# Last image of a four-layer convolution block: the row norms of the next chunk taken first in the output loop, and depthwise taps moved from TensorE to VectorE

## Chip, cores and metric

The kernel runs on one core of one Trainium2 chip. The metric is the device time of one launch in microseconds (us); less is better. All data are float32. The engines are called PE (TensorE, matrix products), DVE (VectorE), ACT (ScalarE), POOL (GpSimd) and SP (SyncE, whose queue issues most of the transfers). Each engine works through its own instructions in the order in which the program hands them over, and semaphores hold an instruction back until what it needs is there.

## What is computed

The input is a batch of 4 images with 256 channels of 64 x 64 pixels. Four layers follow each other, each as x = x + layer(groupnorm(x)):

- layer 0: a 3x3 convolution, then attention over all 4096 pixels of the image;
- layer 1: linear attention with root-mean-square norms at its input and at its output;
- layer 2: a depthwise 3x3 convolution whose nine taps per channel are generated from the image, then a 1x1 convolution with a generated 256 x 256 matrix;
- layer 3: a 1x1 convolution with a mixture of four matrices.

The change touches layers 1 and 2, for the last image only. Cut to what matters there, the reference is:

```python
# layer 1, at its end: w_out times the attended values, then a norm over the channels of each pixel
out = einsum('oc,bchw->bohw', w_out, out) + b_out
n   = sqrt(sum(out * out, axis=1))              # one number for each pixel
x   = x + out / max(n, 1e-12) * g_out * sqrt(256)

# layer 2: u is groupnorm(x); dk has 9 taps for each channel, pk is 256 x 256
dw = depthwise_conv_3x3(u, dk)
x  = x + einsum('bchw,boc->bohw', dw, pk) + bias

# layer 3 begins with groupnorm(x), and so with the mean and variance of what layer 2 wrote
```

## The kernel before, in words

**The whole.** The work of one image is a front (layer 0's convolution and projections), an attention, and a tail (the end of layer 0 and layers 1 to 3). The tail of image b and the front of image b+2 are woven into the attention of image b+1 as generators that are advanced in turns with it. The last image has no attention after it that could hide its tail, so its tail stands alone at the end of the program. Pieces of the last 1x1 convolution of the image before it (`held`, L1676 to L1680) are kept back and issued by `w.fill(n)` at places where the tail leaves PE idle; `w.settle()` issues the additions that belong to them.

**The order.** There is no scheduler: the instructions of each engine stand in the order in which the Python code issues them. Tiles come from rotating pools. All PSUM banks come from one pool of 8 (`bank`), handed out in turn, so a product has to wait until the user of the bank eight requests earlier is done.

**Layer 1's output loop (L1281 to L1338).** The 4096 pixels are taken in 8 chunks of 512. For each chunk:

- `outputs(c)` multiplies four blocks of 128 pixels with the folded output matrix into two banks (PE, L1287), and ACT squares each block and sums it over the channels into a column of `zr` (L1289);
- `root(zr)` bounds the sums from below on DVE (L1294) and raises them to the power -0.5 on POOL (L217, through `rsqrt`);
- `scaled` multiplies the blocks with that root: three on ACT (L1303), the fourth on DVE (L1305), which in the program waits for the third copy of ACT;
- `added(c, z, halves)` transposes the scaled blocks on PE (L1316), and for each half of the channels DVE adds them to the image (recorded at L127, the helper `stt`) and takes statistics (`bn_stats`, L1318).

The loop for the last image is L1322 to L1338. In iteration c it issues `outputs(c+1)`, `scaled` of chunk c, the first half of `added` of chunk c-1, `root` of chunk c+1, and the second half of `added` of chunk c-1. In iterations 2 and 4 one held piece (two products of 512 pixels, one bank) is issued at the end, and the addition to it follows one iteration later. What the loop leaves behind, statistics of the whole image, is needed by everything that follows.

**Layer 2 for the last image (`shared_out`, L1541 to L1591).** The image is cut in 4 chunks of 1024 pixels (16 rows), and the 256 channels in 2 halves; part i is chunk i // 2 and half i % 2. The nine taps of a part are computed in one of two ways:

- on DVE: ACT writes the centre tap (`centre`, L1452), and `taps` (L1481 to L1491) adds eight shifted copies with `stt`, one instruction of 1008 or 1024 elements for each. Parts 0, 2, 4, 6 and 7 are made so.
- on PE: `taps_by_products` (L1493 to L1509) multiplies with nine diagonal matrices (`diag`, written by ACT at L1548), accumulating in a bank of 512 pixels; ACT copies the bank out (L1508). It is a generator that stops after each product. Parts 1, 3 and 5 are made so: 3 parts, 2 banks, 9 products, 54 in all.

When both halves of a chunk are there, `point` issues the 1x1 convolution (PE, L1460, four products for each half of a chunk), and `pointwise_added` adds the result to the image on DVE with a sum (L1476) and squares it on ACT with a sum (L1478). These sums are the statistics from which layer 3 starts (`st()`, L1437). The generated matrix `pk` is put together on DVE by `mix_kernel` (8 instructions of 512 elements, recorded at L127). The order of all this is written out by hand at L1563 to L1591 with `go(i, n)` (n taps of part i on DVE) and `diagonal(n)` (n products on PE).

**Layer 3.** A short chain of small steps gives the mixed matrix `wm`; PE then works off the last three held pieces and 32 products of its own (L1660), and DVE adds and stores each (L1665, L1666).

Of the kernel before, what the change touches and what calls it, by code (L numbers as in the profile page):

```python
# [13 lines left out]
P = 128  # L14
NH = 2
HW = 64
N = HW * HW
CH = 1024
RB = 8
# [74 lines left out]
def conv_preact_fast(ctx: ExitStack, tc: tile.TileContext, guard, x, wc, wtpg, ww, wqkv, wout, w1cat, wd2,  # L94
# [3 lines left out]
    nc = tc.nc  # L98
# [21 lines left out]
    def bank(name):  # L120
        return pp.tile([P, 512], F32, tag="bank", name=name, bufs=8)
# [4 lines left out]
    def stt(o, a, s, b, op0, op1):  # L126
        nc.vector.scalar_tensor_tensor(o, a, s, b, op0, op1)  # L127
# [5 lines left out]
    xp = cp.tile([P, NH, HW + 2, HW], F32, name="xp")  # L133
# [60 lines left out]
    half = cp.tile([P, 8], F32, name="half")  # L194
# [52 lines left out]
    taps = wc_s.rearrange("p h (i j) o -> p h i (j o)", i=3)  # L247
# [913 lines left out]
    def linear_attention(w, b, big, qT, k4, st, sh, sums):  # L1161

        alone = sums is not None
        if alone:
# [80 lines left out]
        last = None  # L1245
        for c in range(NC):
# [10 lines left out]
            last = this  # L1257
# [35 lines left out]
        def root(zr):  # L1293
            nc.vector.tensor_scalar(zr, zr, 1e-24, None, ALU.max)  # L1294
            rsqrt(zr, zr)

        def scaled(zr, banks):
            z = k4("z").rearrange("p (j o) -> p j o", j=4)
            if alone:
                for j in range(4):  # L1300
                    src = banks[j // 2][:, j % 2, :]
                    if j < 3:
                        nc.scalar.activation(z[:, j, :], src, AF.Copy, scale=zr[:, j:j + 1])  # L1303
                    else:
                        nc.vector.tensor_scalar(z[:, j, :], src, zr[:, j:j + 1], None, ALU.mult)  # L1305
                return z
            for s in range(2):
                tt(z[:, bass.ts(s, 2), :], banks[s], zr[:, bass.ts(s, 2)].unsqueeze(2).to_broadcast([P, 2, NH * P]), ALU.mult)
            return z

        def added(c, z, halves=range(NH)):
            cols = bass.ts(c, 512)
            for h in halves:
                pt = bank("ps_zt")
                for j in range(4):
                    nc.tensor.transpose(pt[:, bass.ts(j, P)], z[:, j, bass.ts(h, P)], ident)  # L1316
                stt(big[:, h, cols], pt, gains[:, 1, h:h + 1], big[:, h, cols], ALU.mult, ALU.add)
                nc.vector.bn_stats(st[:, h, c, :], big[:, h, cols])  # L1318

        if alone:  # L1320

            this, last = outputs(0), None  # L1322
            root(this[0])
            for c in range(NC):
                after = outputs(c + 1) if c + 1 < NC else None
                z = scaled(*this)
                for h in range(NH):
                    if last is not None:
                        added(c - 1, last, (h,))
                    if h == 0 and after is not None:  # L1330
                        root(after[0])
                this, last = after, z
                w.settle()
                if c in (2, 4):
                    w.fill(1)
                yield 1
            added(NC - 1, last)
            w.fill(2)  # L1338
            return st

        last = None
        for c in range(NC):
# [5 lines left out]
            last = scaled(*zb)  # L1348
# [9 lines left out]
    TAPS = [(i, j) for i in range(3) for j in range(3) if (i, j) != (1, 1)]  # L1358

    def generated(w, b, big, k4, st, sh, diag):  # L1360
# [108 lines left out]
        def pointwise_added(c, res):  # L1469
            cols = bass.ts(c, 512)  # L1470
            for oh in range(NH):
                if diag is None:
                    tt(big[:, oh, cols], res[oh], big[:, oh, cols], ALU.add)
                    nc.vector.bn_stats(st[:, oh, c, :], big[:, oh, cols])
                else:
                    nc.vector.scalar_tensor_tensor(big[:, oh, cols], res[oh], 1.0, big[:, oh, cols], ALU.mult, ALU.add,  # L1476
                                                   accum_out=sums[:, 0, oh, c:c + 1])
                    nc.scalar.activation(junk(), big[:, oh, cols], AF.Square, bias=pivot[:, oh:oh + 1],  # L1478
                                         accum_out=sums[:, 1, oh, c:c + 1])

        def taps(i):  # L1481

            c, h = PARTS[i]
            dst = dw[i].rearrange("p (y x) -> p y x", x=HW)
            for ty, tx in TAPS:
                dx = tx - 1
                x0, x1 = max(0, -dx), min(HW, HW - dx)
                k = h * 9 + 3 * ty + tx
                stt(dst[:, :, x0:x1], xp[:, h, c * rows + ty:c * rows + ty + rows, x0 + dx:x1 + dx], dk[:, k:k + 1],
                    dst[:, :, x0:x1], ALU.mult, ALU.add)  # L1490
                yield 0.62  # L1491

        def taps_by_products(parts):  # L1493

            for i in parts:
                c, h = PARTS[i]
                dw[i] = k4("dw")
                for s in range(2):
                    ps = bank("ps_dw")
                    dst = ps.rearrange("p (y x) -> p y x", x=HW)  # L1500
                    for n, (ty, tx) in enumerate([(1, 1)] + TAPS):
                        dx = tx - 1
                        x0, x1 = max(0, -dx), min(HW, HW - dx)
                        y0 = (2 * c + s) * RB + ty
                        nc.tensor.matmul(dst[:, :, x0:x1], diag[:, 3 * ty + tx, :], xp[:, h, y0:y0 + RB, x0 + dx:x1 + dx],  # L1505
                                         start=(n == 0), stop=(n == 8))
                        if n == 8:
                            nc.scalar.copy(dw[i][:, bass.ts(s, 512)], ps)  # L1508
                        yield  # L1509

        def mix_kernel(slices, js):

            for j in js:
                stt(pk, slices[j // 2][:, j % 2, :], pb[:, R + j:R + j + 1], pk, ALU.mult, ALU.add)
# [26 lines left out]
        def shared_out():  # L1541

            slices = [load_wp2(j) for j in range(R // 2)]
            yield from w.pending()
            products = taps_by_products([2 * c + 1 for c in range(N // CH - 1)])
            dw[0] = centre(0)
            for k in range(9):
                nc.scalar.activation(diag[:, k, :], ident, AF.Copy, scale=dk[:, 9 + k:10 + k])  # L1548
            on_vector = {i: taps(i) for i in (0, 2, 4, 6, 7)}

            def go(i, n):
                for _ in range(n):
                    next(on_vector[i])

            def diagonal(n):
                for _ in range(n):
                    next(products)

            def point(c):
                d = [dw[2 * c + h] for h in range(NH)]  # L1560
                return [(2 * c + s, pointwise_products(s, d)) for s in range(2)]

            dw[2] = centre(2)  # L1563
            diagonal(24)
            go(0, 8)
            w.settle()
            mix_kernel(slices, range(0, R // 2))
            go(2, 3)
            mix_kernel(slices, range(R // 2, R))
            go(2, 5)  # L1570
            dw[4] = centre(4)
            res = point(0)
            diagonal(12)
            pointwise_added(*res[0])
            go(4, 1)
            pointwise_added(*res[1])
            go(4, 7)
            dw[6], dw[7] = centre(6), centre(7)
            res = point(1)
            diagonal(18)  # L1580
            go(6, 1)
            pointwise_added(*res[0])
            go(6, 2)
            pointwise_added(*res[1])
            go(6, 5)
            go(7, 8)
            res = point(2)
            pointwise_added(*res[0])
            res = res[1:] + point(3)
            for r in res:  # L1590
                pointwise_added(*r)  # L1591

        if diag is None:
            yield from in_order(range(len(PARTS)))
# [752 lines left out]
```

## Time and profile before

| | |
|---|---|
| three timed executions | 3084.27, 3085.98 and 3086.03 us, median 3085.98 |
| the profiled execution | 3084.23 us, of which the profile's span is 3082.4 us |
| busy share of the span | PE 97%, DVE 69%, ACT 38%, POOL 4% |
| granted TensorE clock over the span | 0.993 |
| output loop of the last image | 2899.17 us (first product) to 2941.91 us (first step after its statistics) |
| depthwise stage of the last image | 2954.15 us (first centre tap) to 3033.55 us (end of its last square) |
| products of layer 3 and end | from 3039.41 us |

A row of the profile names the source line, the engine, the operation, and the tiles that it writes and reads. Operations issued by a helper carry the helper's line: L127 is `stt`, L124 is `tt`, L217 is `rsqrt`. A float32 product appears as two records of PE, so "x48" in a row of PE is 24 products; a transpose is one record. The chain of waits follows the work that ended last backwards from its end: at each step it goes to what released the instruction, or to the instruction ahead of it on the same engine. In the rows of the stages, each engine's busy time in a stretch is followed by its count of instructions, and PEclk is the TensorE clock that was granted.

### The profile page before, as it was taken

The numbers are of one execution on the slowest core, as the hardware profiler recorded it, in microseconds if no ns is written. First come the engines' busy times: TensorE is split into PE (matmuls) and PEld (weight loads), VectorE is DVE, ScalarE is ACT, GpSimd is POOL, SyncE is SP. The second block draws the span as 40 slices with busy tenths as digits, with TensorE's granted clock in tenths as the row PEclk, the third lists the DMA queues.
The fourth block names the chain that finished last, engine by engine and source line by source line (L and its number), as shares of the span: only waits on it lengthen the run. The fifth ranks groups of instructions, "written<-read, shape, count | busy, mean of one in ns | idle before, by whom it ended". The sixth has DMA issues, their size and how long they took to land.

```text
span 3082.4 us, 24468 instructions
## 1 busy us (share of the span) xinstructions
PE 3000.3 (97%) x8606; PEld 1483.7 (48%) x8606; DVE 2128.5 (69%) x2780; ACT 1162.0 (38%) x2155; POOL 132.1 (4%) x178
## 2 busy tenths in 40 slices
PE   6899999999999999999999999999999999999998
PEld 3454555445554444444565444444546544444643
DVE  8747777853547996777536797678563569876485
ACT  2334333353555332223364532222436453334621
POOL 0100000000010000000011000000001100000100
PEclk9999999999999999999999999999999999999999
DMA  5233111122100023113300102311420000022021
GB/s 219 84 101 137 34 48 32 34 52 73 57 11 28 14 75 122 39 40 66 116 1 11 35 7 82 123 45 38 96 82 14 18 28 28 14 82 89 8 69 66
DMA packets 61089, 178.45 MB, mean 58 GB/s; under 512 B 6560, under 2 KB 16544, under 8 KB 56736
## 3 DMA queue, kind: packets, MB, share of 16 engines
q1 hardware_dynamic: 56928, 160.04, 15.1%
q0 software_dynamic: 4032, 16.78, 2.9%
q8 instruction: 70, 1.15, 0.2%
q14 instruction: 59, 0.48, 0.1%
HBM read 115.45 MB, written 78.12 MB: 63 GB/s over the span
## 4 chain that ended last, share of the span: by engine, by line
PE 77%; DVE 16%; issue 5%; ACT 1%; POOL 0%; DMA 0%; POOLq 0%; DVEq 0%; ACTq 0%
PE pf L984 22%; PE py L1040 22%; PE ps_qkv L1201 5%; PE ps_conv L512 4%; PE ps_tp L926 4%; DVE dw L127 4%; PE ps_ex L1660 4%; DVE tot L124 3%; PE ps_pw L1460 3%; PE ps_conv L584 2%; PE ps_g L931 2%; PE ps_wy L1021 2%; PE ps_o L1287 1%; PE ps_dw L1505 1%; DVE big L127 1%
## 5 line engine op out<-in xcount | busy, mean ns | idle before, releaser
L985 ACT ACTIVATE pr<-pf 128x512 f32<-128x512 f32 x1024 | 603.9, 597 | 1195.4 <-PE pf L984 1147.9
L984 PE MATMUL pf<-tpg 128*128 128x512 f32 x2048 | 968.9, 595 | 2.9 <-ACT pr L985 2.9
L1040 PE MATMUL py<-pr,tpg 128*128 128x512 f32 x2048 | 962.3, 592 | 2.5 <-ACT pr L985 2.3
L124 DVE TENSOR_TENSOR tot<-tot,pr 128x1024 f32<-128x1024 f32 x448 | 546.3, 1219 | 174.1 <-ACT pr L985 172.5
L1040 PEld LDWEIGHTS py<-pr,tpg 128*128 128x128 f32 x2048 | 388.6, 190 | 494.6 <-issue 477.6
L984 PEld LDWEIGHTS pf<-tpg 128*128 128x128 f32 x2048 | 382.0, 190 | 438.4 <-issue 412.6
L127 DVE SCALAR_TENSOR_TENSOR dw<-xp,dk,dw 128x1008 f32<-128x1008 f32 x208 | 263.0, 1268 | 9.9 <-ACT dw L1452 7.0
L512 PE MATMUL ps_conv<-v,u 128*128 128x512 f32 x384 | 171.0, 593 | 3.6 <-DVE v L124 3.6
L1201 PE MATMUL ps_qkv<-wqkv_s,xg 128*128 128x384 f32 x384 | 129.9, 487 | 0.0
L124 DVE TENSOR_TENSOR tpg<-ps_g,bg_s 128x512 f32<-128x512 f32 x32 | 22.1, 692 | 145.2 <-PE ps_g L931 145.2
L926 PE MATMUL ps_tp<-big,wtpg_s 128*128 128x512 f32 x256 | 117.7, 603 | 3.0 <-ACT big L684 3.0
L512 PEld LDWEIGHTS ps_conv<-v,u 128*128 128x128 f32 x384 | 72.6, 190 | 96.5 <-issue 89.8
L217 POOL TENSOR_TENSOR rstd<-rstd,half 128x2 f32<-128x2 f32 x24 | 17.6, 731 | 2342.1 <-DVE rstd L365 2225.2
L1013 DVE RECIPROCAL inv<-pss 128x512 f32<-128x512 f32 x31 | 103.9, 3352 | 5.5 <-PE pss L996 5.5
L1460 PE MATMUL ps_pw<-dw,pk 128*128 128x512 f32 x224 | 101.3, 592 | 0.0
L1201 PEld LDWEIGHTS ps_qkv<-wqkv_s,xg 128*128 128x128 f32 x384 | 72.2, 190 | 53.6 <-issue 9.8
L1220 DVE TENSOR_REDUCE qs<-qk 128x16 f32<-128x512 f32 x24 | 16.5, 686 | 117.4 <-ACT qk L1214 117.4
L927 ACT ACTIVATE tpg<-ps_tp,btp_s 128x512 f32<-128x512 f32 x64 | 43.8, 687 | 119.2 <-PE ps_tp L926 119.2
L926 PEld LDWEIGHTS ps_tp<-big,wtpg_s 128*128 128x128 f32 x256 | 47.8, 194 | 54.9 <-issue 50.4
L1289 ACT ACTIVATE junk<-ps_o 128x256 f32<-128x256 f32 x128 | 49.2, 385 | 63.9 <-PE ps_o L1287 56.3
L1214 ACT ACTIVATE qk<-ps_qkv,rinv 128x256 f32<-128x256 f32 x96 | 45.6, 475 | 72.4 <-PE ps_qkv L1201 60.0
L124 DVE TENSOR_TENSOR v<-ra 128x1024 f32<-128x1024 f32 x58 | 69.5, 1220 | 0.4
(369 smaller groups left out, 3132.7 us busy)
## 6 DMA issues: line engine op xcount, KB each, us to landing
xp<-in_x_dram SPq DMA_DIRECT2D x16, 1024.0 KB, 6.3
wy_d<-wt SPq DMA_DIRECT2D x32, 512.0 KB, 3.0
wy<-wy_d SPq DMA_DIRECT2D x32, 512.0 KB, 4.9
out_dram<-res SPq DMA_DIRECT2D x64, 256.0 KB, 2.0
xs_d<-big POOLq DMA_DIRECT2D x24, 512.0 KB, 11.1
u<-filters SPq DMA_DIRECT2D x48, 256.0 KB, 2.5
xs<-xs_d SPq DMA_DIRECT2D x24, 512.0 KB, 6.1
u<-rows_d SPq DMA_DIRECT2D x36, 256.0 KB, 3.1
```

What stands on the lines that cost most here:

```text
L124: nc.vector.tensor_tensor(o, a, b, op)
L127: nc.vector.scalar_tensor_tensor(o, a, s, b, op0, op1)
L512: nc.tensor.matmul(ps[oh], u(oh, h), v[:, bass.ts(h, 512)], start=(h == 0), stop=(h == NH - 1))
L584: nc.tensor.matmul(ps[:, bass.ts(oh, IY * IX)], u[i][:, h, bass.ts(oh, P)], v[:, i, bass.ts(h, IY * IX)], start=(h == 0), stop=(h == NH - 1))
L926: nc.tensor.matmul(ps, wtpg_s[:, h, k, :], big[:, h, cols], start=(h == 0), stop=(h == NH - 1))
L984: nc.tensor.matmul(pf, phi[:, bass.ts(2 * m + s, P)], theta[:, bass.ts(q, 512)], start=True, stop=True)
L985: nc.scalar.activation(pr[:, bass.ts(s, 512)], pf, AF.Exp)
L1013: nc.vector.reciprocal(inv, pss)
L1040: nc.tensor.matmul(py, g[:, bass.ts(2 * m + s, P)], probs[i][:, bass.ts(s, 512)], start=(m == 0 and s == 0), stop=(m == NM - 1 and s == 1))
L1201: nc.tensor.matmul(ps[:, 0:3 * HID], xg[:, h, bass.ts(j, P)], wqkv_s[:, h, :], start=(h == 0), stop=(h == NH - 1))
L1460: nc.tensor.matmul(ps, pk[:, h * NH * P + oh * P:h * NH * P + (oh + 1) * P], dw[h][:, bass.ts(s, 512)], start=(h == 0), stop=(h == NH - 1))
L1660: nc.tensor.matmul(ps, wm[h][:, bass.ts(oh, P)], big[:, h, bass.ts(c, 512)], start=(h == 0), stop=(h == NH - 1))
```

## The change

It has two parts, both in the tail of the last image.

In the output loop `root` of chunk c+1 is issued directly after `outputs(c+1)`, ahead of `scaled` of chunk c, and both halves of `added` of chunk c-1 follow together.

In the depthwise stage

- part 1 is made by PE from the centre and six taps, and its last two taps are added by DVE (`go(1, 2)`); PE so has 50 diagonal products in place of 54, and the calls of `diagonal` ask for 27, 5 and 18 in place of 24, 12 and 18;
- part 7 is made by DVE in two pieces of 8 rows (8 instructions of 504 or 512 elements for each piece) in place of 8 instructions of 16 rows;
- the last chunk's 1x1 products are issued one channel half and one piece at a time (`half(s, h)`): three of the four groups ahead of the second piece's taps in the program, the fourth after them; the additions of chunk 2's first half are issued between the two pieces, those of its second half after them.

```diff
             for c in range(NC):
                 after = outputs(c + 1) if c + 1 < NC else None
+                if after is not None:
+                    root(after[0])
                 z = scaled(*this)
-                for h in range(NH):
-                    if last is not None:
-                        added(c - 1, last, (h,))
-                    if h == 0 and after is not None:
-                        root(after[0])
+                if last is not None:
+                    added(c - 1, last)
                 this, last = after, z
...
-        def taps(i):
+        def taps(i, some=TAPS, over=slice(0, CH // HW)):
 
             c, h = PARTS[i]
-            dst = dw[i].rearrange("p (y x) -> p y x", x=HW)
-            for ty, tx in TAPS:
+            dst = dw[i].rearrange("p (y x) -> p y x", x=HW)[:, over, :]
+            for ty, tx in some:
...
-            products = taps_by_products([2 * c + 1 for c in range(N // CH - 1)])
+            products = taps_by_products([(1, TAPS[:6]), (3, TAPS), (5, TAPS)])
...
-            on_vector = {i: taps(i) for i in (0, 2, 4, 6, 7)}
+            on_vector = {i: taps(i) for i in (0, 2, 4, 6)}
+            on_vector[1] = taps(1, TAPS[6:])
...
             dw[2] = centre(2)
-            diagonal(24)
+            diagonal(27)
             go(0, 8)
             w.settle()
             mix_kernel(slices, range(0, R // 2))
             go(2, 3)
             mix_kernel(slices, range(R // 2, R))
+            go(1, 2)
             go(2, 5)
             dw[4] = centre(4)
             res = point(0)
-            diagonal(12)
+            diagonal(5)
...
             go(6, 5)
-            go(7, 8)
+
+            ends = [taps(7, TAPS, slice(s * RB, (s + 1) * RB)) for s in range(2)]
+            for _ in ends[0]:
+                pass
             res = point(2)
+            banks = [[bank("ps_pw") for _ in range(NH)] for _ in range(2)]
+
+            def half(s, h):
+                for oh in range(NH):
+                    nc.tensor.matmul(banks[s][oh], pk[:, h * NH * P + oh * P:h * NH * P + (oh + 1) * P],
+                                     dw[6 + h][:, bass.ts(s, 512)], start=(h == 0), stop=(h == NH - 1))
+
+            half(0, 0)
+            half(0, 1)
+            half(1, 0)
             pointwise_added(*res[0])
-            res = res[1:] + point(3)
-            for r in res:
-                pointwise_added(*r)
+            for _ in ends[1]:
+                pass
+            half(1, 1)
+            pointwise_added(*res[1])
+            for s in range(2):
+                pointwise_added(6 + s, banks[s])
```

More of the change, by code (lines that the diff above doesn't have):

```diff
@@ L1488, in taps @@
                 k = h * 9 + 3 * ty + tx
-                stt(dst[:, :, x0:x1], xp[:, h, c * rows + ty:c * rows + ty + rows, x0 + dx:x1 + dx], dk[:, k:k + 1],
+                y = c * rows + ty
+                stt(dst[:, :, x0:x1], xp[:, h, y + over.start:y + over.stop, x0 + dx:x1 + dx], dk[:, k:k + 1],
                     dst[:, :, x0:x1], ALU.mult, ALU.add)
@@ L1493, in taps_by_products @@
         def taps_by_products(parts):
-            for i in parts:
+            for i, some in parts:
                 c, h = PARTS[i]
@@ L1500, in taps_by_products @@
                     dst = ps.rearrange("p (y x) -> p y x", x=HW)
-                    for n, (ty, tx) in enumerate([(1, 1)] + TAPS):
+                    for n, (ty, tx) in enumerate([(1, 1)] + some):
                         dx = tx - 1
@@ L1505, in taps_by_products @@
                         nc.tensor.matmul(dst[:, :, x0:x1], diag[:, 3 * ty + tx, :], xp[:, h, y0:y0 + RB, x0 + dx:x1 + dx],
-                                         start=(n == 0), stop=(n == 8))
-                        if n == 8:
+                                         start=(n == 0), stop=(n == len(some)))
+                        if n == len(some):
                             nc.scalar.copy(dw[i][:, bass.ts(s, 512)], ps)
```

## The prediction, made before the changed kernel was run

> **What bounds the kernel now.** I read the share of busy time first, then the last 180 us in stretches, because the change lies only there, and then the chain of waits and the engines' timelines inside the stretches. PE is busy for 97% of the span, but not evenly:
>
> ```profile
> 2900.00:2925.00 25.00, 22.41 (x104) 15.64 (x103) 14.09 (x28) 18.65 (x71) 5.95 (x6) 1.00 0.06 22
> 2925.00:2950.00 25.00, 18.42 (x86) 9.49 (x86) 19.44 (x43) 7.78 (x23) 2.86 (x5) 0.80 0.11 37
> ...
> 2975.00:3000.00 25.00, 25.00 (x60) 11.18 (x59) 21.86 (x26) 4.97 (x12) 0.00 (x0) 1.00 0.00 1
> 3000.00:3025.00 25.00, 25.00 (x60) 11.05 (x60) 23.92 (x29) 6.67 (x14) 0.00 (x0) 1.00 0.00 0
> ```
>
> The columns are the stretch, its length, and busy time of PE, weight loads, DVE, ACT and POOL. In the output loop (2899 to 2942) no engine is full. In the depthwise stage (2954 to 3033) PE is full, and DVE nearly so. The chain of waits names the loop's cause:
>
> ```profile
> 2928.31 0.08 DVE zr L1294
> ...
> 2928.55 1.02 POOL zr L217
> ...
> 2929.59 1.22 ACT rt L1303 x3
> ...
> 2930.91 0.48 DVE rt L1305
> 2931.39 0.67 DVE tpg L127
> ...
> 2932.08 0.69 DVE st L1318
> 2932.78 0.08 DVE zr L1294
> ```
>
> This is a ring through four engines: root on DVE to POOL 0.30, POOL and handing on 1.04, ACT's three copies up to DVE's fourth 1.31, that copy 0.40, the addition 0.78, the statistics 0.61, then the next root: 4.46 per chunk. It closes only because the root stands on DVE behind the previous chunk's copy and addition.
>
> In the depthwise stage the timelines of DVE and ACT show:
>
> ```profile
> 3000.65 1.27 DVE L127 SCALAR_TENSOR_TENSOR dw<-xp,dk,dw 128x1008 f32<-128x1008 f32 x1 [3.33 <-ACT dw L1452]
> ...
> 3013.19 10.43 DVE L127 SCALAR_TENSOR_TENSOR rt<-xp,dk,rt 128x1008 f32<-128x1008 f32 x8
> ...
> 3031.63 0.69 DVE L1476 SCALAR_TENSOR_TENSOR tpg<-ps_pw,tpg 128x512 f32<-128x512 f32 x1 [1.02 <-PE ps_pw L1460]
> ```
>
> DVE once waits 3.33 for a centre tap, which stands on ACT behind the copy of PE's part 3 (2995.74) and four squares; and its last additions wait for PE, 1.02 each. So PE ends this stage.
>
> [...] the centre tap above waits 3.33 us behind work it doesn't need. [...] a chained addition of 512 elements takes 3.02 / 4 = 0.755 (the `pk` row, 2968.32 to 2971.34), one of 1008 or 1024 takes 10.35 / 8 = 1.294. [...] 0.50 granted from 2930.8 to 2941.0 and from 3036.6 to 3043.4.
>
> **Part 1, the root first.** No instruction is added; POOL gets its eight powers earlier, and no DMA moves past anything. The ring opens: root c+1 needs only the squares of chunk c+1. New on DVE is the wait: the fourth copy of chunk c and both additions of chunk c-1 now stand behind root c+1, hence behind those squares, and the transposes and later banks wait for these. Three limits are left. DVE alone: 4.46 less its idle 1.14, about 3.24 to 3.3 per chunk (plus 0.66 where a held piece is added). ACT alone: four squares 2.03 and three copies 1.09, 3.12. And banks: a chunk's products start when an addition two chunks back frees a bank. The trace has that sequence once: products 2921.99, squares 2923.10, copies 2925.13, fourth copy 2926.44, that is 4.45; from there to the end of the second addition 2.54; 7.0 for two chunks, 3.5 each. A held piece puts 1.72 of PE ahead of the next products.
>
> The walk of the fourth copies, from chunk 1 (2908.62, unchanged, since ACT was busy with squares until then):
> - chunk 2: DVE-bound, +3.2, 2911.9.
> - chunk 3: its squares wait for products of chunk 4, which follow the held piece (ends 2911.64): squares from 2912.8, copies 2914.7, 2916.0.
> - chunk 4: DVE-bound with a held addition, +3.9, 2919.9.
> - chunk 5: the second held piece waits for a copy of chunk 4 (2918.65); products 2920.4, squares 2921.5, copies 2923.5, 2924.8.
> - chunk 6: +3.9, 2928.7. Chunk 7: +3.2, 2931.9.
>
> Before, chunk 7 was at 2935.37; what follows (6.5 to the last statistics) keeps its shape. Gain 3.5. Ends: 5.5 if all of DVE's six waits go (1.11, 1.14, 0.49, 1.14, 0.49, 1.14); 1.4 if PE's clock halves inside the loop (rival below).
>
> **Part 2, the depthwise stage.** PE: 54 products took 20.39 + 10.19 + 15.29 = 45.87, 0.85 each; four fewer are 3.4 less. DVE gets two taps more (2.55 net of overlap 2.45), and 16 half taps at 0.755 (12.0) for 8 at 1.294 (10.35), 1.6 more. No trace row has half taps of 8 rows; the `pk` row is the nearest in length and chaining. From below 0.65 (half a full tap), from above 1.29 (no cheaper than a full one). I take 0.755.
>
> Walked in the old trace's times (part 1 only shifts them). PE: 27 products end at 2981.0; the first 1x1 needs part 1's two taps, done on DVE at 2980.7: no wait, but the cover is only 0.3, beyond which a late DVE costs one for one. 1x1 to 2987.9, 5 products to 2992.1, 1x1 to 2999.0, 18 products to 3014.2, 1x1 of chunk 2 to 3021.1, three groups of the last chunk to 3026.3. DVE: the two taps push it to 2999.8 where it waited for the centre tap; ACT, now freed 3.4 earlier, has that ready at 2997.5, so the wait of 3.33 is gone: DVE runs 0.9 ahead and starts part 7 at 3012.3. First piece 3018.3, two additions 3019.5, second piece 3025.4. PE's last group runs 3026.3 to 3028.0, so PE no longer ends the stage. DVE's six last additions run 3025.4 to 3029.1 without waiting. Next late is ACT: six squares at 0.845 from 3026.2 (0.78 after the first addition starts, as at 3023.54), end 3031.3. Before: 3033.55. Gain 2.25. The other instructions (copies, centres, squares) keep number and order; moved squares are hidden under PE's products, and would cost at most their 0.85 each.
>
> **After it.** Layer 3's chain (3033.55 to 3039.41) and PE's last products shift unchanged: the mixed matrix is ready at 3044.4, PE reaches it at 3046.6 behind held pieces. PE idles 8 to 9 us there in both kernels, so its clock halves in both[...]. Output transfers (2.0 us to landing) follow as before; the loads of `pk`'s slices land ten us ahead of use.
>
> **Sum.** 3084.23 (span 3082.4 and 1.8 around it) - 3.5 - 2.25 = 3078.5. The profiled execution is 1.75 below the median of the timed ones; the four executions lie in two pairs, near 3084.25 and 3086.0. I lift the sum to their middle, 0.9: 3079.4.
>
> **Rivals.**
> - All of DVE's waits in the loop go (5.5): 3077.4. For it: ACT's 3.12 is below DVE's 3.3. Against: banks and held pieces. 0.12.
> - PE's clock halves inside the loop: two-chunk sequence 1.3 longer, 4.2 per chunk against 4.46, gain 1.4: 3081.5. For it: 0.50 was granted from 2930.8 on. Against: PE's work is denser now. 0.13.
> - The depthwise part gives nothing, ACT's squares or a missed cover of 0.3 taking the place of PE: 3081.6. For it: DVE and PE are both full. 0.10.
> - Slower: half taps cost as much as full ones[...]. Then 16 x (1.294 - 0.755) = 8.6 more on DVE, which ends the stage: 3088.0. It decides above 0.755 + 5.75 / 16 = 1.11 per half tap. Against: 0.755 for 512 elements. 0.05; that the stage slips by still more is 0.03 of these.
> - As worked out: 0.60, half above the line drawn next.
>
> **How the numbers follow.** A measurement of this kernel can tell about 0.2%, 6.2 us, so the line is 3079.8; the forecast lies 0.4 below it. Faster by more: 0.12 + 0.33 = 0.45. Within: 0.27 + 0.13 + 0.10 + 0.02 = 0.52. Slower by more: 0.03. The range leaves out the slow rival and the far ends: 3076.0 to 3083.5.
>
> **What would show it.** Right: roots no longer in the chain of waits for each chunk; fourth copies 3.2 to 4.9 apart; DVE without the wait at the centre tap of part 6; the last squares back to back on ACT, and PE ending before them; half taps near 0.755. Wrong: a PE wait ahead of the first 1x1, DVE's idle at a root, or half taps above 0.9.

## The result: 3081.7 us against 3086.1

| | before | after |
|---|---|---|
| median of the executions (20 each) | 3086.07 us | 3081.71 us |
| lowest and highest | 3083.42, 3086.70 | 3079.36, 3082.43 |
| the profiled execution, and its span | 3084.23, 3082.4 | 3079.89, 3078.1 |

The ratio is 0.9986, 95% interval 0.9980 to 0.9993: 4.4 us less. The executions of each kernel lie in two groups about 2.4 apart, before near 3083.8 and 3086.2, after near 3079.7 and 3082.0. Both medians fall in the upper group and both profiled executions in the lower one, so medians and profiles compare like with like.

The stretches of the changed kernel that answer to those of before (stretch, its length, then busy time of PE, weight loads, DVE, ACT and POOL, the granted clock, DMA):

```profile
2900.00:2925.00 25.00, 23.34 (x110) 16.76 (x108) 15.00 (x31) 20.06 (x77) 7.05 (x7) 1.00 0.06 22
2925.00:2950.00 25.00, 19.55 (x90) 9.43 (x89) 21.01 (x48) 8.06 (x20) 1.75 (x3) 0.86 0.26 80
2975.00:3000.00 25.00, 25.00 (x60) 11.05 (x59) 24.57 (x30) 6.64 (x12) 0.00 (x0) 1.00 0.00 1
3000.00:3025.00 25.00, 24.55 (x58) 10.64 (x56) 24.36 (x39) 8.00 (x19) 0.00 (x0) 1.00 0.00 0
```

In the depthwise stage DVE went from 21.86 to 24.57 busy in 25 us: its wait is gone. PE is for the first time not full there, 24.55 in the last row: it is done before the stage ends.

The chain of waits in the loop of the changed kernel (start, time, what; "x3" are three instructions):

```profile
2923.36 1.10 ACT z L1303 x3
...
2924.56 0.48 DVE z L1305
2925.04 0.67 DVE tpg L127
...
2927.73 0.73 DVE res L127
2928.46 0.08 DVE zr L1294
2928.54 0.39 DVE rt L1305
```

POOL's root is gone from it. Before, it stood in the chain in the last two turns (2928.55 and 2933.01), and ACT's copies waited for it, 1.34 or more, in five of the six turns from chunk 2 on. The root on DVE (L1294) now takes its 0.08 in passing, between two pieces of DVE's own work. What stays is DVE's own sequence, and ACT's copies where a held piece came first.

DVE's timeline of the changed kernel, in the loop and in the depthwise stage (start, busy time, and in brackets the idle time ahead of the instruction and what ended it):

```profile
2911.69 0.15 DVE L1294 TENSOR_SCALAR zr<-zr 128x4 f32<-128x4 f32 x1
2911.75 0.48 DVE L1305 TENSOR_SCALAR ra<-ps_o,zr 128x256 f32<-128x256 f32 x1
...
2915.85 0.48 DVE L1305 TENSOR_SCALAR z<-ps_o,zr 128x256 f32<-128x256 f32 x1 [0.79 <-ACT z L1303]
...
2924.56 0.48 DVE L1305 TENSOR_SCALAR z<-ps_o,zr 128x256 f32<-128x256 f32 x1 [1.00 <-ACT z L1303]
...
2996.10 1.26 DVE L127 SCALAR_TENSOR_TENSOR dw<-xp,dk,dw 128x1008 f32<-128x1008 f32 x1
...
3015.97 6.21 DVE L127 SCALAR_TENSOR_TENSOR rt<-xp,dk,rt 128x504 f32<-128x504 f32 x8
...
3027.97 0.19 DVE L1436 TENSOR_REDUCE both_m<-sums 128x4 f32<-128x32 f32 x1 [2.04 <-ACT junk L1477]
```

Chunk 2's copy (2911.75) follows its root without a wait; chunks 3 and 5, the ones that stand behind a held piece, wait 0.79 and 1.00. Part 6's first tap (2996.10) has no bracket: the wait of 3.33 is gone. Eight half taps take from 3015.97 to the next addition at 3022.11, 0.767 each. DVE's last 2.04 of idle is ended by ACT: the squares now end the stage.

The gain, followed through the traces by marks that both kernels have (us, before to after):

| mark | before | after | gain so far |
|---|---|---|---|
| fourth copy of chunk 7 | 2935.37 | 2931.61 | 3.76 |
| first centre tap of layer 2 | 2954.15 | 2950.51 | 3.64 |
| last square of layer 2 done (`both_m`) | 3033.55 | 3027.97 | 5.58 |
| first product with the mixed matrix | 3046.62 | 3042.18 | 4.44 |
| last product of PE that both have (`count`) | 3075.99 | 3071.55 | 4.44 |

So 3.64 came from the loop and 1.94 from the depthwise stage, and then 1.14 was given back between the last square and the mixed matrix, where nothing had been changed. PE's timeline there, first before:

```profile
3039.34 7.44 PE L1660 MATMUL ps_ex<-big,wmh 128*128 128x512 f32 x12
3046.62 3.60 PE L1660 MATMUL ps_ex<-tpg,wm 128*128 128x512 f32 x8
```

and after:

```profile
3033.97 8.37 PE L1679 MATMUL ps_ex<-big,wmh 128*128 128x512 f32 x12
3042.18 3.60 PE L1679 MATMUL ps_ex<-tpg,wm 128*128 128x512 f32 x8
```

The same twelve records of the held pieces take 8.37 in place of 7.44. The stretches say why. In both traces the granted clock changes eleven times, each a whole multiple of 3.41 us from the others; a stretch between two such instants is called a window from here on, and the row of instants the grid. Cut at the grid, before:

```profile
3033.22:3036.63 3.41, 0.77 (x4) 0.59 (x4) 1.85 (x13) 0.30 (x2) 0.00 (x0) 1.00 0.01 2
3036.63:3040.04 3.41, 1.80 (x7) 1.49 (x8) 0.93 (x8) 0.35 (x2) 0.70 (x1) 0.50 0.02 5
3040.04:3043.46 3.42, 3.42 (x5) 1.35 (x4) 3.20 (x10) 0.00 (x0) 0.00 (x0) 0.50 0.00 0
```

and after:

```profile
3026.30:3029.71 3.41, 0.38 (x2) 0.30 (x2) 1.09 (x8) 1.61 (x4) 0.00 (x0) 1.00 0.01 2
3029.71:3033.12 3.41, 1.18 (x6) 1.01 (x6) 1.24 (x9) 0.00 (x0) 0.70 (x1) 0.50 0.00 0
3033.12:3036.54 3.42, 3.08 (x5) 1.67 (x6) 2.18 (x9) 0.35 (x2) 0.00 (x0) 0.50 0.03 5
3036.54:3039.95 3.41, 3.41 (x5) 1.35 (x4) 3.11 (x7) 0.00 (x0) 0.00 (x0) 0.50 0.00 0
```

Read the last but two columns (the clock) against the first busy column (PE). Before, half clock covers two windows, of which the held products sit in the second and a little of the first: 4.1 us of slow products. After, PE ends its 1x1 convolution 7.0 us earlier (3024.55 against 3031.60) and the held products begin 5.4 earlier, but the windows of these two profiles stand at the same places, within 0.1. So the products begin 0.85 behind the start of a window in place of 2.71; half clock covers three windows, and the products lie in two of them: 6.0 us slow. The window in which they began, with PE busy for 3.08 of its 3.42, was followed by another at half clock.

### The profile page after: what moved, and what is told of

Same layout as the page of the kernel before. It is cut to its first block, busy times and chain, and to the rows that moved or that the text cites. A ratio compares the mean times of both kernels' runs of the same rounds, so it can differ in the third digit from the quotient of the medians.

```text
span 3078.1 us, 24460 instructions
## 1 busy us (share of the span) xinstructions
PE 2996.4 (97%) x8598; PEld 1482.2 (48%) x8598; DVE 2132.2 (69%) x2790; ACT 1161.6 (38%) x2155; POOL 132.1 (4%) x178
```

## The experiments

Theory: the loop's gain is the opened ring; the depthwise gain is PE's four products and DVE's wait; what is missing was taken by the clock at the restart. Rivals: the two parts overlap, the pieces of part 7 bring the gain, or the restart is slower for another reason.

The edits are shown cut, against the changed kernel where nothing else is said. The kernel before was timed again beside every run, with medians from 3084.59 to 3086.07, depending on how many of its executions fell in either group; the changed kernel was not, so a difference to its 3081.71 of less than about 1.5 says little by itself. The marks in the profiles are the finer measure.

**The root first, alone.** The depthwise stage is as before.

```diff
-            products = taps_by_products([(1, TAPS[:6]), (3, TAPS), (5, TAPS)])
-            on_vector = {i: taps(i) for i in (0, 2, 4, 6)}
-            on_vector[1] = taps(1, TAPS[6:])
+            products = taps_by_products([2 * c + 1 for c in range(N // CH - 1)])
+            on_vector = {i: taps(i) for i in (0, 2, 4, 6, 7)}
...
-            diagonal(27)
+            diagonal(24)
```

> The kernel before with the first part of the change alone. Theory (the two parts add, and what is left over is TensorE's clock at the restart of layer 3): the last fourth copy of the loop near 2931.6 in place of 2935.4, the depthwise stage as long as before (first centre tap to end of the last square 79.4 us), and 3.6 us less than before in all, because the restart falls so in the clock's windows that about 4 us of it are slow, as before. Rival (the first part's gain is given back later): less than 2 us of the 3.7 are left at the end.

Measured: 3082.63, ratio 0.9992 (0.9984 to 1.0001), the kernel before at 3085.49 beside it. Chunk 7's fourth copy at 2931.64, the depthwise stage 79.40 as before, the last product at 3072.46: 3.5 earlier than before. So in the profiles nearly all of the loop's 3.76 arrives when it is alone; half clock at its restart lasts two windows, as before, not three, and the twelve held records take 7.51 (before 7.44, after 8.37). The medians show 2.9, less than the 3.6 expected, with an interval that reaches 1.0001: the rival falls by the marks, not by the times.

**The depthwise part, alone.** The loop is as before.

```diff
-                if after is not None:
-                    root(after[0])
                 z = scaled(*this)
-                if last is not None:
-                    added(c - 1, last)
+                for h in range(NH):
+                    if last is not None:
+                        added(c - 1, last, (h,))
+                    if h == 0 and after is not None:
+                        root(after[0])
```

> The kernel before with the second part of the change alone. Theory: the loop keeps its 4.46 us per chunk; the depthwise stage is 1.9 us shorter; but the restart of layer 3 comes about 0.8 us after a window's begin, the clock stays at half for 6 us in place of 4, and only 1.0 us is left of the 1.9 at the end. Rival (the lost 1.0 us of the changed kernel belongs to the loop or to an interaction of the parts): 1.9 us less than before at the end.

Measured: 3083.15, ratio 0.9996 (0.9987 to 1.0004). The stage takes 77.46, 1.94 shorter, but the last product comes only 1.1 earlier: half clock at the restart lasts three windows (3032.97 to 3043.21), and the held products take 8.28. So of the two it is this part that brings the slower restart in the profiles. The held products begin 1.93 earlier than before, which puts them 1.03 behind the start of a window; with the first part alone they begin 3.59 earlier, about a whole window, and stand 2.58 behind one, nearly as before. The median lies 2.3 below that of the kernel before, but fell in the lower group, the other in the upper; group against group it is about 1, as in the marks.

**The taps moved, part 7 in one piece.** Root first and the two taps on DVE are kept; the ending is the old one.

```diff
-            on_vector = {i: taps(i) for i in (0, 2, 4, 6)}
+            on_vector = {i: taps(i) for i in (0, 2, 4, 6, 7)}
...
-            ends = [taps(7, TAPS, slice(s * RB, (s + 1) * RB)) for s in range(2)]
-            for _ in ends[0]:
-                pass
+            go(7, 8)
             res = point(2)
...
             pointwise_added(*res[0])
...
+            res = res[1:] + point(3)
+            for r in res:
+                pointwise_added(*r)
```

> The changed kernel with part 7 in one piece and the old ending, two taps still on VectorE. Theory A (moving the taps is what pays[...]): walked from the trace of after, VectorE ends part 7 1.4 us sooner than in two pieces, TensorE's last products end near 3025.9, the last square near 3027.9, the same as in two pieces; total within 0.5 us of the changed kernel. Theory B (the pieces are what takes TensorE off the end of the stage): 1.5 to 2 us slower than the changed kernel.

Measured: 3081.31, ratio 0.9983 (0.9976 to 0.9990), in two groups, 3077.3 to 3077.8 and 3080.9 to 3082.0. The stage takes 76.84, 0.6 less than with two pieces. DVE's timeline of this kernel:

```profile
3010.75 10.43 DVE L127 SCALAR_TENSOR_TENSOR rt<-xp,dk,rt 128x1008 f32<-128x1008 f32 x8
...
3027.55 0.69 DVE L1475 SCALAR_TENSOR_TENSOR tpg<-ps_pw,tpg 128x512 f32<-128x512 f32 x1 [1.02 <-PE ps_pw L1459]
```

PE still ends the stage here: the last addition waits 1.02 for it, the one before 0.99. The pieces take those two waits away, 2.0, and cost 16 x 0.767 - 10.34 = 1.9 of DVE, so the last addition starts 74.65 after the first centre tap with them and 74.92 without. But with the pieces ACT still has squares to do when the additions end: the stage ends 2.81 after the last addition's start with them, 1.92 without. The profiled execution fell in the upper group and shows, besides, a window of half clock (2942.04 to 2945.45) over the small products of layer 2 ahead of this stage.

**The pieces, without the moved taps.**

```diff
-            products = taps_by_products([(1, TAPS[:6]), (3, TAPS), (5, TAPS)])
+            products = taps_by_products([(1, TAPS), (3, TAPS), (5, TAPS)])
...
-            diagonal(27)
+            diagonal(24)
...
-            go(1, 2)
             go(2, 5)
...
-            diagonal(5)
+            diagonal(12)
```

> The changed kernel with part 1 made by TensorE alone (54 diagonal products), part 7 in two pieces. Theory A: TensorE has its 3.4 us back and ends the stage again; the stage is about as long as in the kernel before (79.4 us), the total 1.5 to 2 us above the changed kernel unless the restart falls better in the clock's windows. Theory B (the pieces pay): within 0.5 us of the changed kernel.

Measured: 3083.45, ratio 0.9995 (0.9987 to 1.0003). The stage takes 79.79, against 79.40 of before: the pieces by themselves bring nothing, and what the depthwise part gains comes from the moved taps. The twelve held records take 7.23 (before 7.44, after 8.37).

**Warm products at the restart.** Products that nobody reads keep PE busy from its last 1x1 convolution to the held pieces.

```diff
             half(1, 1)
+            warm(512, 512, 512, 512, 512)
...
+    def warm(*widths):
+        ps = bank("ps_warm")
+        for n in widths:
+            nc.tensor.matmul(ps[:, 0:n], ident, tpg[:, NH, 0:n], start=True, stop=True)
...
-        mv, gm, rstd = yield from group_finish(st, avg8, 1e-5, sh)
+        mv, gm, rstd = yield from group_finish(st, avg8, 1e-5, sh,
+                                               (lambda: warm(384), lambda: warm(512, 128)) if held is None else ())
...
+        if held is None:
+            warm(256)
```

> The changed kernel with nine more products into banks that nobody reads, issued where TensorE has nothing to do between the last depthwise product and the restart of layer 3 (five of 512 columns first, then four of 128 to 512 between the small products). Theory (the restart of layer 3 loses half of its 5.9 us at half clock): full clock there, the last held pieces end 2.5 to 3.0 us earlier, total 2.5 to 3 us below the changed kernel. Rival (the restart is bound by the mixed matrix, or the late end comes from something else than the clock): no gain, or a loss of up to 0.5 us from the added products.

Measured: 3080.94, ratio 0.9987 (0.9981 to 0.9994), only 0.8 below the changed kernel. The condition `held is None` holds for the first two images as well, so the products also ran inside the attentions, and the last image's loop starts 4.8 later: the total is no test. The tail is: no half clock (1.00 granted from 3030 to 3042, where the changed kernel has 0.59), held products 5.42, and from the last square to the mixed matrix 10.65 in place of 14.21, so 3.6 us of the restart, as this profile of the changed kernel has it, are the clock's.

**The same in the last image only,** against the run just shown.

```diff
-                                               (lambda: warm(384), lambda: warm(512, 128)) if held is None else ())
+                                               (lambda: warm(384), lambda: warm(512, 128)) if b == B - 1 else ())
...
-        if held is None:
+        if b == B - 1:
             warm(256)
```

> The changed kernel plus unread warm products at the end of the depthwise stage and between the small products of layer 3's chain, in the last image only (five of 512 columns, then 384, then 512 and 128, then 256; their bank is read by nobody). Theory (a slow clock at the restart takes back part of the gain): no half clock from the last square on, the held pieces' twelve products about 5.4 us instead of 8.4, the last square to the mixed-matrix product 10.7 instead of 14.2, and the time about 3.0 to 3.5 below the changed kernel, near 3078.2. Rival (the clock doesn't bind there, or the warm products cost what they bring): within 1 us of 3081.7.

Measured: 3076.66 (11 executions), ratio 0.9975 (0.9966 to 0.9984), 5.0 below the changed kernel. Part of that is which group the median fell in: the groups are 3075.9 to 3076.7 and 3078.8 to 3079.1, so group against group the gain is 3.0 to 3.3, as expected. PE's timeline of this kernel:

```profile
3024.02 4.46 PE L1625 MATMUL ps_warm<-tpg,ident 128*128 128x512 f32 x10
...
3033.00 5.42 PE L1688 MATMUL ps_ex<-big,wmh 128*128 128x512 f32 x12
```

The twelve records take 5.42 against 8.37. The clock is the cause of the slow restart.

**Warm products ahead of layer 2's small products,** on top of the kernel with part 7 in one piece.

```diff
     def generated(w, b, big, k4, st, sh, diag):
-        mv, gm, rstd = yield from group_finish(st, avg8, 1e-5, sh)
+        mv, gm, rstd = yield from group_finish(st, avg8, 1e-5, sh,
+                                               () if diag is None else (lambda: warm(384), lambda: warm(512, 256)))
```

> The kernel with the taps moved and the last part in one piece, plus unread warm products (384, then 512 and 256 columns) between the two small products ahead of layer 2's hidden products, in the last image only. Theory (the window of half clock that stood over those hidden products, 2942.0 to 2945.5, decides which of two clusters an execution falls in): no half clock there, the step from the last statistics to the first centre tap about 2 us shorter than the 13.1 of the slow case, and the executions no longer split between 3077.5 and 3081.5 but lie near 3077.5 to 3078. Rival (the two clusters come from elsewhere, ahead of this image's tail): both clusters stay, 3 to 4 apart, and the median moves by less than 1.

Measured: 3078.42, ratio 0.9977 (0.9968 to 0.9986). The executions run from 3077.07 to 3079.64 with no gap: the group above 3080.9 is gone. This answers the question of the two groups in the main, though the spread is wider than expected.

**Both sets of warm products on the changed kernel** (the two edits above together):

> The changed kernel with both sets of unread warm products of the last image: ahead of layer 2's hidden products and at the restart of layer 3. If the upper of its two clusters of executions (2.4 apart) is half clock over the hidden products, only the lower is left: one cluster near 3076.4, no wider than 2. Rival (the clusters come from elsewhere): two clusters again, near 3076.4 and 3079.0.

Measured: 3076.39, ratio 0.9972 (0.9961 to 0.9984), all executions within 3075.6 and 3076.9. With the restart's products alone there were two groups, 2.6 apart; with the second set there is one, the lower. So it is half clock over layer 2's small products that makes the upper group. The kernel with the taps in one piece shows it,

```profile
2942.59 0.40 PE L1376 MATMUL ps_b<-off,w1n 128*32 128x1 f32 x12 [1.52 <-DVE w1n L124]
2942.80 6.65 PE L1393 MATMUL ps_h<-tpg,w1n 128*32 128x512 f32 x32
```

and this one has at the same place

```profile
2940.76 1.54 PE L1626 MATMUL ps_warm<-tpg,ident 128*128 128x512 f32 x4
...
2942.58 5.32 PE L1394 MATMUL ps_h<-tpg,w1n 128*32 128x512 f32 x31
```

The profile of the kernel in one piece takes 20.63 from chunk 7's fourth copy to the first centre tap, that of the changed kernel, without half clock there, 18.90. That is 1.7 of the distance between the groups; where the rest arises is not shown.

**Both sets on the kernel before** (the first set stands after `point(3)`):

> The kernel before with the same two sets of warm products. It has no wait of PE's clock left, so the change's own gain is this run less the changed kernel with the same products. Theory (the change saves 3.76 in the loop and 1.94 in the depthwise stage, and the slow clock at the restart takes back 1.0): near 3081.4 to 3082, and 5.4 to 5.7 above the changed kernel so treated. Rival (the restart takes back nothing, or something else does): 4.4 above it, as in the plain pair.

Measured: 3082.94, ratio 0.9992 (0.9984 to 1.0001), one group, 3082.1 to 3083.8. It is 6.55 above the changed kernel so treated, and not 4.4. The profiles of the two differ by 5.77 at the last product. Of this 3.64 is there at chunk 7's fourth copy, and 1.95 comes from the depthwise stage (79.40 against 77.45). The treatment itself adds 0.8: here PE ends later, so the five products still run when the statistics are ready, the first small product starts 2.17 after the last square in place of 1.31, and from the last square to the last product it is 40.79 against 40.02. It takes 0.6 off again between the fourth copy and the first centre tap (18.61 against 19.20). So with these two places kept at full clock the change saves 5.6, as the marks of the plain pair said (3.64 and 1.94), against 4.4 where the clock slows there. The medians lie another 0.8 apart, which no mark explains.

**One piece, both sets:**

> The changed kernel with part 7 in one piece and the old product order at the end, with the same two sets of warm products. Theory (sixteen half taps of 0.766 cost 1.9 more than eight whole ones of 1.29, of which a shorter ending gives back 1.3): 0.6 below the changed kernel so treated, near 3075.8. Rival (the 0.6 seen before is the clock's): equal within 0.3.

Measured: 3076.88, ratio 0.9974 (0.9964 to 0.9985): not below the changed kernel so treated (3076.39), but 0.5 above. In the trace the stage is again 0.6 shorter (76.83 against 77.45), and again the warm products hold the small ones up by 0.8, as in the kernel before. The stage's 0.6 is shown twice; that it shortens the whole is not shown, because 0.2 lost by this sum and 0.5 measured are both within the executions' spread of 1.3 to 1.7.

**The held pieces out of the loop.** The loop's two slow turns are those with a held piece. Two of the pieces are moved behind the last 1x1 convolution.

```diff
                 w.settle()
-                if c in (2, 4):
-                    w.fill(1)
                 yield 1
...
             half(1, 1)
+            w.fill(2)
```

> The changed kernel with the two held pieces of the output loop issued after the last depthwise product, where TensorE idles; no work is left out. Theory (in the changed loop the held pieces stand on TensorE ahead of the next chunk's products, and make two of the six steps 4.1 and 4.8 us long): all six steps 3.2 to 3.5 us, the loop 2.0 to 3.0 us shorter, total 2 to 3.5 us below the changed kernel. Rival (banks limit the loop, the pieces are hidden): steps as long as before, total within 0.7 us of the changed kernel.

Measured: 3076.57, ratio 0.9971 (0.9960 to 0.9983), 5.1 below the changed kernel, more than was expected. DVE's timeline of this kernel:

```profile
2915.86 0.15 DVE L1294 TENSOR_SCALAR zr<-zr 128x4 f32<-128x4 f32 x1
2915.92 0.48 DVE L1305 TENSOR_SCALAR z<-ps_o,zr 128x256 f32<-128x256 f32 x1
...
2919.14 0.48 DVE L1305 TENSOR_SCALAR rt<-ps_o,zr 128x256 f32<-128x256 f32 x1
```

Every turn takes 3.16 to 3.23 without a wait, DVE's own work and nothing else; chunks 1 to 7 take 19.27 in place of 23.08. The held pieces fill PE's gap at the restart, where half clock shrinks to one window (0.86 granted from 3030 to 3042, where the changed kernel has 0.59): from the last square to the mixed matrix it is 12.26 in place of 14.21.

**All of it together.** Root first, taps moved, one piece, no held pieces in the loop, both sets of warm products (at the restart one of 512 columns after the two held pieces, then as above).

```diff
-                if c in (2, 4):
-                    w.fill(1)
...
+            res = res[1:] + point(3)
+            w.fill(2)
+            warm(512)
+            for r in res:
+                pointwise_added(*r)
```

> All together: root first, taps moved, last part in one piece, no held pieces inside the output loop (two of them run after the last 1x1 convolution, and a single warm product of 512 columns after them), and warm products of the last image as in the other two. If the parts add up: 3081.7 less 3.8 (loop without held pieces), less 0.6 (one piece), less 3.0 to 3.5 (clock at the restart), near 3074, with a spread of 3072.5 to 3075.5. Rival (they share the same wait: the held pieces fill the restart already, so the warm products bring nothing on top of them): near 3076.5, as with the held pieces moved alone.

Measured: 3072.91, ratio 0.9959 (0.9945 to 0.9972), 3072.0 to 3073.6: 8.8 below the changed kernel and 13 below the one before, faster than both. It is 1.1 below what was expected. The profile is 3.44 shorter at the last product than that of the kernel with the held pieces out of the loop: 1.64 between the fourth copy and the first centre tap, 0.62 in the depthwise stage, 0.84 from the last square to the mixed matrix (11.42 in place of 12.26), and 0.34 ahead of the loop. So the rival was right in part: where held pieces fill the restart already, warm products bring 0.8 there and not 3. The expected sum counted 3.0 to 3.5 for the restart and nothing for layer 2, and that it came near is in part luck.

## Why the prediction was right, point by point

**The time.** 3079.4 was forecast and 3081.71 measured, inside 3076.0 to 3083.5 and on the side of a gain. The number by itself does not tell for the mechanism: two rivals stood at 3081.5 and 3081.6, nearer than the forecast. The traces have to decide. (Of the 0.60 for the way as worked out, called half above the line, 0.33 and 0.27 went into the sums.) Against the kernel before as measured beside it, the sum's 5.75 became 4.36. The loop gave 0.26 more than its term and the depthwise stage 0.31 less, and that these nearly cancel is luck.

**The walk of the loop** held step by step. Fourth copies of chunks 2 to 7 (us):

| chunk | 2 | 3 | 4 | 5 | 6 | 7 |
|---|---|---|---|---|---|---|
| forecast | 2911.9 | 2916.0 | 2919.9 | 2924.8 | 2928.7 | 2931.9 |
| measured | 2911.75 | 2915.85 | 2919.74 | 2924.56 | 2928.45 | 2931.61 |

The waits stand where the walk put them, at chunks 3 and 5, and from chunk 2 on nowhere else except 0.41 at a root (2923.39) ahead of chunk 5's. The gain was 3.76 for 3.5. The two opposed rivals fell with it: neither did all six waits go, nor did half clock reach into the turns before chunk 7 (it begins at 2930.72). That the held pieces set the two long turns was an argument then; the run without them shows it.

**The depthwise part** gave 1.94 for 2.25. Taken from the first centre tap, PE's last group starts at 72.15 in the walk and at 72.16 in the trace; the second piece of part 7 ends at 71.25 and 71.60; the last square ends at 77.15 and 77.46. The miss of 0.3 is there by the end of the second piece: half taps of 0.767 in place of 0.755 are 0.2 of it. ACT ended the stage with six squares back to back, as said. The cover at the first 1x1 convolution, called 0.3, held: DVE ended the two taps at 2977.03 and PE began at 2977.39, without a wait. The slower rival needed 1.11 per half tap and is out.

What the prediction did not ask is which of the part's two edits brings the gain. It is the moved taps alone; the pieces spare DVE 2.0 of waiting for PE and cost it 1.9, and the stage is 0.6 longer with them, by ACT's squares.

**The step that was off in its size** is "After it": the restart was taken to shift unchanged, with half clock in both kernels. Half clock stood there in both, two windows before and three after, and the restart cost 1.14 more, 0.93 in the held products and 0.2 in the small ones. PE's gap was misread as 8 to 9 in both kernels: from its last 1x1 product to the held pieces it was 7.7 before and 9.4 after. But the longer gap is not what costs. The kernel with one piece has the old gap ahead of the first small product (3.27, before 3.26), and the slow restart,

```profile
3030.78 0.59 PE L348 MATMUL pm<-mv,avg 128*128 128x2 f32 x2 [3.27 <-DVE mv L124]
...
3035.67 8.06 PE L1664 MATMUL ps_ex<-big,wmh 128*128 128x512 f32 x12
```

and with the warm products ahead of layer 2, which leave its ending as it is, the same gap and a short one:

```profile
3030.07 0.38 PE L348 MATMUL pm<-mv,avg 128*128 128x2 f32 x2 [3.27 <-DVE mv L124]
...
3034.68 7.17 PE L1670 MATMUL ps_ex<-big,wmh 128*128 128x512 f32 x12
```

What goes with the cost in all seven profiles without warm products or held pieces at the restart is the place in its window at which the held products begin. Half clock from there is, within 0.1, twice what their twelve records exceed the 5.42 of full clock (us):

| kernel | gap ahead of the first small product | held products begin behind the window's start | half clock from there | the twelve held records | last square to mixed matrix |
|---|---|---|---|---|---|
| after | 4.73 | 0.85 | 5.98 | 8.37 | 14.21 |
| depthwise part alone | 4.73 | 1.03 | 5.80 | 8.28 | 14.12 |
| one piece | 3.27 | 1.47 | 5.35 | 8.06 | 14.10 |
| root first alone | 3.27 | 2.58 | 4.24 | 7.51 | 13.15 |
| before | 3.26 | 2.71 | 4.12 | 7.44 | 13.07 |
| pieces without the taps | 3.66 | 3.12 | 3.70 | 7.23 | 12.92 |
| one piece, warm ahead of layer 2 | 3.27 | 3.27 | 3.56 | 7.17 | 12.92 |

The grid does not stand at the same place in all profiles: it does within 0.3 in those of before, after and the two parts alone, by chance as far as is known, and in the kernel with one piece it stands 1.08 later than in the changed kernel. So a trace of the kernel before could not give the sign. What stays open is why the timed executions of the plain pair, not only the profiled ones, are 4.4 apart and not 5.6; only one execution of each kernel was profiled.

**The lift of 0.9** for the place of the profiled execution was too small: it belonged to the lower of two groups, and the median fell in the upper, 2.4 above, in both kernels.

## What to carry to other kernels

When an edit moves the place at which PE starts again after a phase of small dependent steps, look at the clock there: the same work took from 12.9 to 14.2 us, by where in a window it began, and this took back 1.1 of 5.6 in the two profiles. A filler that nobody waits for (held work, or products that nobody reads) placed in that gap was worth 3 us, against 4.4 for the whole change; but it must end before the first small step is ready, or it costs what it overlaps (0.8 us in the kernel before). Work put into a loop "where an engine has room" can stand in the way of the next turn's first product: the two held pieces cost 3.8 us in the loop and nothing at the restart.

## What the runs showed of the hardware

- In the profiles of before and after, the granted clock is 1.00 or 0.50, and its eleven changes in each lie whole multiples of 3.41 us apart (0.50, for instance, for 3.41 us at 589.27 before, for 10.24 at 135.30 and 2930.82). The grid's place is not the same in every profile: half clock over a window begins at 2942.04 in the kernel with one piece, where the changed kernel's grid has 2940.96. With the same gap of 3.27 the restart took 14.10 and 12.92 (one piece, without and with the warm products ahead of layer 2).
- In the kernel in one piece, a window with PE recorded busy for 1.61 of 3.42 us (2938.62 to 2942.04) was followed by half clock, and so were windows with 1.53 busy (before, from 2927.41, ahead of the half clock at 2930.8 that the prediction names), 1.72 and 1.93 (after, from 2927.31 and from 2824.91); windows with 1.67 and 1.80 busy (after from 3022.88, before from 3029.80) were not. So the windows ahead of half clock were not all idle, and no limit in recorded busy time parts these two sets.
- A window at half clock with PE recorded busy for 3.08 of 3.42 us (after, 3033.12) was followed by another at half clock, and one with 2.86 (one piece, 2942.04) by full clock. In the profiles of before and after, PE was recorded busy throughout in five windows at half clock in each, and full clock followed all ten.
- A chained addition over 8 rows of 63 or 64 pixels takes 0.767, hardly more than the 0.755 of one over 512 elements of `pk`.
